# A two-image state-space scan: image 0 weighted by C on VectorE and summed with identity products, image 1 with its states transposed to tokens

## The chip, the cores and the metric

The kernel runs on one core of a Trainium2 chip. A core has five engines with an instruction queue each: TensorE (PE, matrix products; its weight loads are listed as PEld), VectorE (DVE), ScalarE (ACT), GpSimd (POOL) and SyncE (SP, which here only issues DMA transfers). An engine works through its queue in order: an instruction that waits holds up everything behind it on that engine. Data lies in SBUF (128 partitions); products land in PSUM, which has 8 banks of 128 x 512 floats and which POOL does not read here. The metric is device time in microseconds (us), the median over several runs. Everything is float32.

## The reference

The network takes x of shape (2, 128, 64, 64): two images, 128 channels, 4096 positions. In order: a group of deformable convolutions with a fuse convolution (called L0 conv below), a router with 8 experts (L0 FFN), a selective-scan mixer (L1 conv) and a last expert layer (L1 FFN). The change lies in the mixer's scan. For each image, with 256 inner channels d, 16 states n and positions t = 0..4095, the scan is

```
h[d,n,t] = exp(delta[d,t] * A[d,n]) * h[d,n,t-1] + delta[d,t] * u[d,t] * B[n,t]
y[d,t]   = sum over n of  C[n,t] * h[d,n,t]   +  D[d] * u[d,t]
out      = (y * gate[d,t]) projected from 256 to 128 channels, added to the layer's input
```

u and the gate come from convolutions of the normalised input; delta, B and C are products of u with small matrices.

## The kernel before

**Pieces and units.** The scan works on pieces of LC = 512 positions: 8 pieces per image, 16 in all. One unit is one scan instruction: 128 channels (one of two halves) by 512 positions for one state n. A piece has 2 x 16 = 32 units, and the loop in `scan` (L1550 onwards) goes over 512 units, ordered by (piece, half, state). Units 0 to 255 are image 0, units 256 to 511 image 1.

**One unit u.** ScalarE makes the decay `da` = exp(delta * A) into a PSUM bank (L1587, two units ahead, two banks). A DMA on SP's queue copies one row of B, broadcast over 128 partitions, to `bcb` (L1598, 256 KB, 8 buffers, about six units ahead). POOL makes the drive `db` = du * bcb (L1580, three units ahead). VectorE runs the scan `h` = scan(da, db) from the kept state (L1668); POOL then copies the last column of h to the state (L1677, one unit later). To weight h by C and sum over n, h is turned so that positions lie on the partitions: `turn` makes four 128 x 128 transposes on TensorE into a PSUM bank `ht` (listed under the helper's line L120, one unit later). There C[n, t] is one number per partition, and `weigh` multiplies it in two units later: for image 0, VectorE takes the first two blocks of 128 in one instruction (L1614) and ScalarE the other two (L1616, one each); for image 1, VectorE one block, ScalarE three. `add` then transposes the four blocks back, summing them in a PSUM bank `py` (L1625, three or four units later). The sum begins with the product of diag(D) and u (L1622). When all 16 states are in, `gate` multiplies by the gate on VectorE (L1637), and `project` (L1700 onwards) does the output projection.

**Preparing a piece.** While a piece is scanned, `prepare` makes the next one's delta, du, gate and rows of B and C in small steps, two steps per unit. It is a generator; `gap(n)` is n empty steps. It uses all engines, and loads xc, zc and sab through SP's queue.

**What lies beside the scan.** The order of the work is written out by hand: each engine's instructions are issued in the order in which the Python code makes them. During image 0's units, a second generator `rest` makes image 1's remaining earlier work: the fuse convolution (units 0 to 34, L875 and L877), the FFN (units 35 to 97, L1028, L1035 and L1044), the mixer's convolutions (units 98 to 190, L1234, L1247, L1269) and channel statistics (units 191 to 225, L1326). After each unit a fixed amount of `rest` is issued, so which step lies beside which unit is fixed by weights in the code. Image 1's units have only the preparation of the next piece and weight loads for the last layer beside them.

**Memory.** PSUM during the scan: two banks `da`, two `ht`, one `py`, and three shared by everything else (tag `m`). SBUF pools are stacked; work tiles of prepare share the tag `wk` with three buffers, and `xr` of project uses it too.

Of the kernel before, what the change touches and what calls it, by code (L numbers as in the profile page):

```python
# [19 lines left out]
P = 128  # L20
B = 2
# [189 lines left out]
class L0Conv:  # L211
# [690 lines left out]
    def residual(self, b, g, keep, sp):  # L902

        nc, cut = self.env.nc, slice(g * 512, (g + 1) * 512)
        row = lambda name: sp.tile([P, 512], F32, name=name, tag="t", bufs=7)
        xr, fa, fn = row("xr"), row("fa"), row("fn")
        nc.sync.dma_start(out=xr, in_=self.env.d["x"][b, :, cut])
        nc.sync.dma_start(out=fa, in_=self.fd[b][:, cut])
        for _ in range(3):
            yield  # L910
        for py in range(2):
            nat = view(fn, py * W, [(2 * W, 4), (2, 32), (1, 2)])
            phases = view(fa, py * 256, [(32, 4), (1, 32), (P, 2)])
            nc.scalar.activation(nat, phases, AF.Relu, bias=keep[:, 1:2], scale=keep[:, 0:1])
        yield
        yield
        return xr, fn


class L0Ffn:  # L920
# [26 lines left out]
    def group(self, b, g, residual, norm, x2, sp, pp):  # L947
        env, nc = self.env, self.env.nc
        bank = lambda shape, name: pp.tile(shape, F32, name=name, tag="m")
        row = lambda name: sp.tile([P, GT, C], F32, name=name, tag="t", bufs=7)  # L950
# [132 lines left out]
BCB = 8  # L1083
# [31 lines left out]
class L1Conv:  # L1115
# [315 lines left out]
    def taps(self, b, k, xc, xs, zz, sa, sp, bank, wk):  # L1431

        env, nc, halves = self.env, self.env.nc, range(2)
        if k == 0:
            self.wd = self.room().tile([P, 2, 4, P], F32, name="wd")
            for h in halves:
                for t in range(4):
                    nc.scalar.mul(self.wd[:, h, t, :], env.ident, self.w1[b][:, h, t : t + 1])
                yield
# [27 lines left out]
    def prepare(self, b, k, sp, pp, res):  # L1467
# [17 lines left out]
        yield from gap(11)  # L1485
        zz = sp.tile([P, 2, LC], F32, name="zc")
# [5 lines left out]
        xs = sp.tile([P, 2, LC], F32, name="xs")  # L1492
        if b:
            yield from self.taps(b, k, xc, xs, zz, sa, sp, bank, wk)
        else:
            yield from self.tap_sums(b, xc, xs, zz, sa, wk)
# [7 lines left out]
        bc = self.dp.tile([DS, LC], F32, name=f"bc{b}_{k}", tag=f"bc{b}_{k}")  # L1504
        nc.sync.dma_start(out=bc, in_=xd[8 : 8 + DS, :])
        res.update(bc=bc)
        yield
        pt = bank([P, GT, 40], "pt")
        for j in range(GT):
            nc.tensor.transpose(pt[:, j, :], xd[:, j * P : (j + 1) * P], env.ident[0:40, 0:40])  # L1510
        yield
        ct = sp.tile([P, GT, DS], F32, name="ct")
        nc.scalar.copy(ct, pt[:, :, 8 + DS :])
        res.update(ct=ct)
# [36 lines left out]
    def scan(self, sp, ps, pp, rest, ahead):  # L1551
# [20 lines left out]
        units = [(k, half, n) for k in range(B * NK) for half in range(2) for n in range(DS)]  # L1572
        pieces, das, dbs, rows, hs, hts, ws = {0: res}, {}, {}, {}, {}, {}, {}

        def drive(u):

            if u < len(units):
                k, half, n = units[u]
                dbs[u] = sp.tile([P, LC], F32, name="db", bufs=AHEAD + 1)
                nc.gpsimd.tensor_tensor(dbs[u], pieces[k]["du"][:, half, :], rows.pop(u), ALU.mult)  # L1580

        def decay(u):
            if u < len(units):
                k, half, n = units[u]
                das[u] = ps.tile([P, LC], F32, name="da")
                dl = pieces[k]["dl"][:, half, :]
                nc.scalar.activation(das[u], dl, AF.Exp, scale=self.A[:, half, n : n + 1])  # L1587

        fetched = 0

        def fetch(u):
            nonlocal fetched
            while fetched <= min(u, len(units) - 1):
                k, half, n = units[fetched]
                if "bc" not in pieces.get(k, {}):
                    break
                rows[fetched] = sp.tile([P, LC], F32, name="bcb", bufs=BCB)
                nc.sync.dma_start(out=rows[fetched], in_=pieces[k]["bc"][n].partition_broadcast(P))  # L1598
                fetched += 1

        adds, py = deque(), {}

        def turn(u):
            hts[u] = ps.tile([P, GT, P], F32, name="ht")
            h = hs.pop(u)
            transpose4(nc, env.ident, hts[u], [h[:, j * P : (j + 1) * P] for j in range(GT)])

        def weigh(u):
            k, half, n = units[u]
            ct, ht = pieces[k]["ct"], hts.pop(u)  # L1610
            ws[u] = sp.tile([P, GT, P], F32, name="w", bufs=4)
            cut = 2 if k < NK else 1
            by = ct[:, 0:cut, n : n + 1].to_broadcast([P, cut, P])
            nc.vector.tensor_tensor(ws[u][:, 0:cut, :], ht[:, 0:cut, :], by, ALU.mult)  # L1614
            for j in range(cut, GT):
                nc.scalar.activation(ws[u][:, j, :], ht[:, j, :], AF.Copy, scale=ct[:, j, n : n + 1])  # L1616

        def add(u):
            k, half, n = units[u]
            if n == 0:  # L1620
                py[k] = ps.tile([P, LC], F32, name="py", bufs=1)
                nc.tensor.matmul(py[k], dg[:, half, :], pieces[k]["xs"][:, half, :], start=True, stop=False)  # L1622
# [11 lines left out]
        def gate(u):  # L1634
            k, half, n = units[u]
            y = pieces[k]["zz"][:, half, :]
            nc.vector.tensor_tensor(y, y, py.pop(k), ALU.mult)  # L1637
# [4 lines left out]
        def flush(u):  # L1642
            while adds and adds[0][0] <= u:
                adds[0][1](adds.popleft()[2])
# [7 lines left out]
        for u, (k, half, n) in enumerate(units):  # L1652
            state = states[k // NK]
            if k and half == 0 and n == 5:
                side.todo.appendleft(project(k - 1))
            last = n == DS - 4 and half == 1
# [6 lines left out]
            fetch(u + BCB - 2)  # L1663
            if k >= NK and u % 24 == 12:
                ahead()

            hs[u] = sp.tile([P, LC], F32, name="h", bufs=3)
            nc.vector.tensor_tensor_scan(  # L1668
                hs[u], das.pop(u), dbs.pop(u), state[:, half, n : n + 1], ALU.mult, ALU.add
            )  # L1670
            if last:
                side.drain()
                fetch(u + BCB - 2)
            drive(u + AHEAD)

            if keep:
                nc.gpsimd.tensor_copy(*keep)  # L1677
            keep = state[:, half, n : n + 1], hs[u][:, LC - 1 : LC]
            decay(u + 2)
            if u:  # L1680
                turn(u - 1)
            if u > 1:
                weigh(u - 2)
            flush(u)
            adds.append((u + (4 if n == 0 else 3), add, u))
            if n == DS - 1:
                adds.append((u + 4, gate, u))
# [12 lines left out]

    def project(self, b, k, ys, sp, pp):

        nc = self.env.nc
        xr = sp.tile([P, 2, LC], F32, name="xr", tag="wk", bufs=3)[:, 0, :].rearrange("p (j c) -> p j c", j=GT)
# [19 lines left out]
    def run(self, after, ahead):  # L1724
# [4 lines left out]
        with (  # L1729
            tc.tile_pool(name="scs", bufs=2) as sp,  # L1730
            tc.tile_pool(name="scp", bufs=2, space=PSUM) as ps,
            tc.tile_pool(name="scm", bufs=3, space=PSUM) as pp,
        ):
            self.dtw = sp.tile([8, 256], F32, name="dtw", bufs=1)
# [250 lines left out]
def metaformer_kernel(ctx: ExitStack, tc: tile.TileContext, d: dict, out: bass.AP):  # L1985
# [6 lines left out]
    with tc.manual_schedule(engines={ET.PE, ET.DVE, ET.Activation, ET.Pool, ET.SP}), ExitStack() as l0:  # L1992
        mixer = L1Conv(env, dp, keep, x2, x3)
        mixer.room = lambda: ctx.enter_context(tc.tile_pool(name="wd", bufs=1, side="right"))
# [104 lines left out]
```

## Time and profile before

| | us |
|---|---|
| median of 7 runs | 7614.09 (7600.16 to 7626.24) |
| the profiled execution | 7606.2 |
| its span on the core | 7604.4 |
| from the span's start to the first scan | 5775.5 |
| image 0's units 0 to 255 | 1015.2 |
| image 1's units 256 to 511 | 562.4 |
| after the last scan's start | 251.3 |

The times in the profile are from the span's start. A group of instructions is named by line, engine, operation and tiles; "busy" is the time in which it ran, "idle before" the time for which the engine stood still just before it, with the instruction that ended the wait. "A <- B" in a list of waits means that A waited for B, with the total time, the number of waits and the longest. A float32 product of 512 columns appears as two records on TensorE, a transpose of 128 columns as one.

The first 5700 us hold the deformable convolutions of both images, with POOL's gathers, and are not touched except for one buffer count (the FFN's shared row tiles).

### The profile page before, as it was taken

To read this page: it belongs to the slowest core of one execution; us is meant where nothing else is said; L and a number is where in the kernel's file an instruction comes from. 1 tells how busy PE (TensorE), PEld (TensorE's weight loads), DVE (VectorE), ACT (ScalarE), POOL (GpSimd) and SP (SyncE) were. 2 spreads that over 40 slices of the span, in tenths; PEclk is the share of its full clock that TensorE was granted. 3 is DMA by queue.
4 is the path that set the end of the run, shared out by engine and by line. 5 is a ranking of instruction groups with operands and counts; after the bars stand their busy time and mean duration, and the time that the engine had idled before them with its cause. 6 is when DMAs were issued, how large, how long until landed. Compare 5 with 4: busy or idle time off the path is not lost.

```text
span 7604.4 us, 72120 instructions
## 1 busy us (share of the span) xinstructions
PE 5227.2 (69%) x22497; PEld 3287.0 (43%) x22497; DVE 5808.8 (76%) x6710; ACT 2248.1 (30%) x4642; POOL 5056.3 (66%) x5062
## 2 busy tenths in 40 slices
PE   4677677777777775756666776666556788867778
PEld 3444444444444442323333453434223567755544
DVE  5878788888888887788888877777875777578782
ACT  1211111111111111311111221111116776768770
POOL 3767677777777777777777776766774344567850
PEclk8887788888888887888888887778777888888889
DMA  7886767776777767877777777777765224455444
GB/s 215 261 278 210 215 210 217 210 223 204 222 213 217 217 207 249 281 230 211 227 213 218 230 223 234 217 242 214 232 203 188 98 91 130 133 153 158 157 149 155
DMA packets 667321, 1550.06 MB, mean 204 GB/s; under 512 B 181668, under 2 KB 230988, under 8 KB 666940
## 3 DMA queue, kind: packets, MB, share of 16 engines
q0 software_dynamic: 307200, 1006.88, 43.9%
q1 hardware_dynamic: 330812, 490.87, 20.6%
q10 hardware_dynamic: 28928, 47.70, 1.7%
q8 instruction: 182, 2.98, 0.2%
q14 instruction: 199, 1.63, 0.1%
HBM read 1436.70 MB, written 110.84 MB: 204 GB/s over the span
## 4 chain that ended last, share of the span: by engine, by line
PE 43%; issue 18%; another core or an unknown queue 15%; ACT 8%; DVE 8%; POOL 4%; DMA 3%; SPq 1%; ACTq 0%; DVEq 0%; POOLq 0%
PE out L799 18%; PE pst L120 6%; PE po L428 6%; POOL v L731 2%; PE ps L1247 2%; ACT st L779 2%; POOL db L1580 2%; DVE v L772 2%; DVE h L1668 1%; PE ps L1234 1%; PE pfo L875 1%; ACT w L1616 1%; PE px L1028 1%; PE ht L120 1%
## 5 line engine op out<-in xcount | busy, mean ns | idle before, releaser
L731 POOL DMA_INDIRECT v<-table,idx x3840 | 4059.2, 1057 | 1619.6 <-issue 1048.8
L772 DVE TENSOR_TENSOR v<-v,pw 128x2048 f32<-128x2048 f32 x960 | 2192.2, 2284 | 612.8 <-DMA v<-table,idx 408.9
L799 PE MATMUL out<-st,regw 128*128 128x512 f32 x3840 | 2234.4, 707 | 244.7 <-issue 189.7
L779 ACT COPY st<-pst 128x512 f32<-128x512 f32 x960 | 556.0, 586 | 4378.1 <-remote 2190.5
L120 PE MATMUL pst<-ident,v 128*128 128x128 f32 x3840 | 720.2, 312 | 1076.4 <-issue 863.5
L774 DVE TENSOR_TENSOR v<-v 128x1024 f32<-128x1024 f32 x960 | 1176.8, 1226 | 33.0
L799 PEld LDWEIGHTS out<-st,regw 128*128 128x128 f32 x3840 | 790.2, 228 | 905.7 <-issue 841.8
L120 PEld LDWEIGHTS pst<-ident,v 128*128 128x128 f32 x3840 | 514.8, 160 | 1460.1 <-issue 1192.0
L1580 POOL TENSOR_TENSOR db<-du,bcb 128x512 f32<-128x512 f32 x512 | 669.5, 1308 | 515.8 <-DVE h L1668 388.1
L1668 DVE TENSOR_TENSOR_SCAN h<-da,state,db 128x512 f32<-128x512 f32 x512 | 652.6, 1275 | 85.9 <-ACT da L1587 52.4
L775 DVE TENSOR_TENSOR v<-v 128x512 f32<-128x512 f32 x960 | 664.3, 692 | 33.0
L120 PE MATMUL ht<-ident,h 128*128 128x128 f32 x2048 | 365.1, 307 | 237.4 <-ACT w L1616 209.1
L428 PE MATMUL po<-wa,win 128*128 128x147 f32 x2112 | 388.9, 306 | 114.8 <-issue 112.2
L428 PEld LDWEIGHTS po<-wa,win 128*128 128x128 f32 x2112 | 340.7, 205 | 231.9 <-issue 231.3
L1587 ACT ACTIVATE da<-delta,w_A_log 128x512 f32<-128x512 f32 x512 | 359.7, 703 | 228.6 <-DVE h L1668 225.2
L120 PEld LDWEIGHTS ht<-ident,h 128*128 128x128 f32 x2048 | 263.0, 157 | 367.2 <-ACT w L1616 302.7
L1616 ACT ACTIVATE w<-ht,ct 128x128 f32<-128x128 f32 x1280 | 383.9, 371 | 22.4 <-DVE w L1614 22.4
L1614 DVE TENSOR_TENSOR w<-ht,ct 128x256 f32<-128x256 f32 (+1 forms) x512 | 174.3, 340 | 230.9 <-PE ht L120 229.1
L1625 PE MATMUL py<-ident,w 128*128 128x128 f32 x2048 | 340.8, 297 | 0.0
L1234 PE MATMUL ps<-ipw,hs 128*120 128x128 f32 x1408 | 212.8, 309 | 151.3 <-ACT X L1181 98.4
L1234 PEld LDWEIGHTS ps<-ipw,hs 128*120 128x120 f32 x1408 | 199.1, 215 | 205.1 <-ACT X L1181 115.5
L1625 PEld LDWEIGHTS py<-ident,w 128*128 128x128 f32 x2048 | 276.3, 157 | 23.6 <-issue 23.3
(327 smaller groups left out, 5294.2 us busy)
## 6 DMA issues: line engine op xcount, KB each, us to landing
bcb<-bc SPq DMA_DIRECT2D x512, 256.0 KB
regw<-in_regw SPq DMA_DIRECT2D x192, 640.0 KB
v<-table,idx POOLq DMA_INDIRECT x3840
yd<-ys ACTq DMA_DIRECT2D x128, 256.0 KB
yc<-yd SPq DMA_DIRECT2D x16, 2048.0 KB
wt<-in_weight SPq DMA_DIRECT2D x32, 1024.0 KB
tm<-pos SPq DMA_DIRECT2D x32, 720.0 KB
pos<-zero SPq DMA_DIRECT2D x48, 240.0 KB
```

What stands on the lines that cost most here:

```text
L120: nc.tensor.transpose(ps[:, j, :], s, ident)
L428: m()
L731: self.env.nc.gpsimd.indirect_dma_start(out=v[:, j, :], out_offset=None, in_=self.table[b], in_offset=bass.IndirectOffsetOnAxis(ap=idx[:, ...
L772: nc.vector.tensor_tensor(v4, v4, w, ALU.mult)
L774: nc.vector.tensor_tensor(up, up, v4[:, :, 2:4, :], ALU.add)
L775: nc.vector.tensor_tensor(v4[:, :, 0, :], v4[:, :, 0, :], v4[:, :, 1, :], ALU.add)
L779: nc.scalar.copy(st, pt.rearrange("p j t -> p (j t)"))
L799: nc.tensor.matmul(self.out[half], self.regw[t // CH][:, t % CH, half * P : (half + 1) * P], st, start=first, stop=last,)
L1234: nc.tensor.matmul(ps[:, k, :], patch, own[o], start=True, stop=True)
L1580: nc.gpsimd.tensor_tensor(dbs[u], pieces[k]["du"][:, half, :], rows.pop(u), ALU.mult)
L1625: nc.tensor.matmul(py[k][:, j * P : (j + 1) * P], w[:, j, :], env.ident, is_transpose=True, start=False, stop=n == DS - 1 and j == GT - 1,)
L1668: nc.vector.tensor_tensor_scan(hs[u], das.pop(u), dbs.pop(u), state[:, half, n : n + 1], ALU.mult, ALU.add)
```

## The change

- **Units of image 0** are ordered (piece, state, half), so that both halves of a state follow each other; image 1 keeps (piece, half, state).
- **Image 0's weighting.** The scan writes its result over `da`, in PSUM. VectorE multiplies it by a broadcast row of C into an SBUF tile `sc` (6 buffers), and TensorE adds it to `py` with one 512-column product by the identity, two units later. The turn, the weighing and the transposes back are gone for image 0; two sums (one per half) run side by side. The state is copied by ScalarE, since it is read from PSUM.
- **Image 1's weighting** is as before.
- **PSUM tags.** `da` has a third bank in image 0 (tag `y`, which is image 1's `py`); image 0's two `py` and image 1's two `ht` share the tag `x`.
- **bcb** becomes a tile of two rows (512 KB, 5 buffers): B and C of one state for image 0, used by both halves, and B of two states for image 1. One transfer serves two units. For image 0, prepare stores both B and C (two small transfers), and no longer makes `ct`.
- **Prepare** starts 5 steps earlier (`gap(6)` for `gap(11)`). `zc` has a third buffer for image 1; `xs` has one buffer per pool; a pool `scx` for image 1's extra tiles is opened when its first piece is prepared. `project` is put in one unit earlier for pieces up to 8, and `xr` has a buffer of its own.
- The tile `h` of image 1 has 6 buffers (before 3), `w` 5 (before 4); the FFN's row tiles 8 (before 7). `wd` moves from its own pool to the scan's.

```diff
-        row = lambda name: sp.tile([P, GT, C], F32, name=name, tag="t", bufs=7)
+        row = lambda name: sp.tile([P, GT, C], F32, name=name, tag="t", bufs=8)
...
-BCB = 8
+BCB = 5
...
-        yield from gap(11)
-        zz = sp.tile([P, 2, LC], F32, name="zc")
+        yield from gap(6)
+        own = self.own(b, sp)
+        third = b and k % 3 == 2
+        zz = (own if third else sp).tile([P, 2, LC], F32, name="zc", bufs=1 if third else 2)
...
-        xs = sp.tile([P, 2, LC], F32, name="xs")
+        xs = (own if k % 2 else sp).tile([P, 2, LC], F32, name="xs", bufs=1)
...
-        bc = self.dp.tile([DS, LC], F32, name=f"bc{b}_{k}", tag=f"bc{b}_{k}")
-        nc.sync.dma_start(out=bc, in_=xd[8 : 8 + DS, :])
+        bc = self.dp.tile([DS, LC] if b else [DS, 2, LC], F32, name=f"bc{b}_{k}", tag=f"bc{b}_{k}")
+        if b:
+            nc.sync.dma_start(out=bc, in_=xd[8 : 8 + DS, :])
+        else:
+            for s in range(2):
+                nc.sync.dma_start(out=bc[:, s, :], in_=xd[8 + s * DS : 8 + (s + 1) * DS, :])
...
-        units = [(k, half, n) for k in range(B * NK) for half in range(2) for n in range(DS)]
+        units = [(k, n, half) for k in range(NK) for n in range(DS) for half in range(2)]
+        units += [(k, n, half) for k in range(NK, B * NK) for half in range(2) for n in range(DS)]
+        first = NK * 2 * DS
...
-                das[u] = ps.tile([P, LC], F32, name="da")
+                third = u < first and u % 3 == 2
+                das[u] = ps.tile([P, LC], F32, name="da", tag="y" if third else "da", bufs=1 if third else 2)
...
-                rows[fetched] = sp.tile([P, LC], F32, name="bcb", bufs=BCB)
-                nc.sync.dma_start(out=rows[fetched], in_=pieces[k]["bc"][n].partition_broadcast(P))
+                bcb[i] = sp.tile([P, 2, LC], F32, name="bcb", bufs=BCB)
+                bc = pieces[k]["bc"]
+                nc.sync.dma_start(out=bcb[i], in_=(bc[n : n + 2] if k >= NK else bc[n]).partition_broadcast(P))
...
+        def start(k, half, key, tag, bufs):
+            py[key] = ps.tile([P, LC], F32, name="py", tag=tag, bufs=bufs)
+            nc.tensor.matmul(py[key], dg[:, half, :], pieces[k]["xs"][:, half, :], start=True, stop=False)
+
+        def identity(u):
+            k, n, half = units[u]
+            nc.tensor.matmul(py[k, half], env.ident, scs.pop(u), start=False, stop=n == DS - 1)
...
-            hs[u] = sp.tile([P, LC], F32, name="h", bufs=3)
-            nc.vector.tensor_tensor_scan(
-                hs[u], das.pop(u), dbs.pop(u), state[:, half, n : n + 1], ALU.mult, ALU.add
-            )
+            s = das.pop(u)
+            h = s if u < first else sp.tile([P, LC], F32, name="h", tag="sc", bufs=6)
+            nc.vector.tensor_tensor_scan(h, s, dbs.pop(u), state[:, half, n : n + 1], ALU.mult, ALU.add)
...
             if keep:
-                nc.gpsimd.tensor_copy(*keep)
-            keep = state[:, half, n : n + 1], hs[u][:, LC - 1 : LC]
+                keep()
+            to, end = state[:, half, n : n + 1], h[:, LC - 1 : LC]
+            keep = functools.partial(nc.scalar.copy if u < first else nc.gpsimd.tensor_copy, to, end)
             decay(u + 2)
-            if u:
-                turn(u - 1)
-            if u > 1:
-                weigh(u - 2)
+            if u < first:
+                scs[u] = sp.tile([P, LC], F32, name="sc", bufs=6)
+                nc.vector.tensor_tensor(scs[u], h, bcb[i][:, 1, :], ALU.mult)
+                if now == 0:
+                    adds.extend((u + 3, start, k, h, (k, h), "x", 2) for h in range(2))
+                adds.append((u + (3 if now == 0 else 2), identity, u))
+                if n == DS - 1:
+                    adds.append((u + 4, gate, k, half, (k, half)))
+            else:
+                if u == first:
+                    flush(u + 4)
+                hs[u] = h
+                if u > first:
+                    turn(u - 1)
+                if u > first + 1:
+                    weigh(u - 2)
+                adds.append((u + (4 if n == 0 else 3), back, u))
...
-        xr = sp.tile([P, 2, LC], F32, name="xr", tag="wk", bufs=3)[:, 0, :].rearrange("p (j c) -> p j c", j=GT)
+        xr = sp.tile([P, GT, C], F32, name="xr", bufs=1)
```

## The prediction

> **What bounds the kernel now.** I read the instruction groups, then busy time by stretch, the waits of image 0's stretch, and two timelines. Only the scan, 5775 to 7353 us, is changed much, so I cut there: fuse convolution (units 0 to 34), FFN (35 to 97), convolutions (98 to 190), statistics (191 to 225), image 0's scan without the other work (226 to 255), image 1's scan, the rest.
>
> ```profile
> L1668 DVE TENSOR_TENSOR_SCAN h<-da,state,db 128x512 f32<-128x512 f32 x512 | 652.6, 1275 | 85.9 <-ACT da L1587 52.4
> ...
> L1614 DVE TENSOR_TENSOR w<-ht,ct 128x256 f32<-128x256 f32 (+1 forms) x512 | 174.3, 340 | 230.9 <-PE ht L120 229.1
> ```
>
> The scan itself rarely stands still; the weighting behind it waits 229 us for the transposes.
>
> ```profile
> 5775.50:5908.00 132.50, 103.40 (x416) 57.71 (x417) 80.42 (x118) 109.30 (x194) 69.81 (x83) 0.90 0.59 203
> 5908.00:6227.50 319.50, 251.26 (x1218) 169.61 (x1216) 238.34 (x498) 241.18 (x542) 126.67 (x149) 0.84 0.26 86
> 6227.50:6577.20 349.70, 299.99 (x2290) 264.10 (x2290) 216.78 (x234) 246.31 (x525) 180.66 (x221) 0.84 0.46 127
> 6577.20:6708.80 131.60, 96.68 (x813) 87.97 (x810) 88.36 (x116) 81.36 (x186) 69.46 (x86) 0.88 0.59 166
> 6708.80:6790.70 81.90, 57.36 (x292) 41.46 (x293) 59.08 (x83) 56.34 (x120) 52.55 (x70) 0.76 0.41 133
> 6790.70:7353.10 562.40, 408.31 (x2394) 301.76 (x2392) 448.55 (x584) 460.32 (x1136) 454.63 (x564) 0.85 0.49 156
> ```
>
> Columns: stretch, length, busy time of PE, PEld, DVE, ACT, POOL, granted clock, DMA share, GB/s. No engine is full. TensorE is nearest in the convolutions (300 of 350); in the FFN PE, ACT and DVE are within 13 us of each other. These stretches lose time by engines waiting for one another. Image 0's waits:
>
> ```profile
> POOL db L1580 <- DVE h L1668: 325.5, 114, 8.6
> DVE w L1614 <- PE ht L120: 174.8, 87, 8.7
> ACT da L1587 <- DVE h L1668: 157.7, 78, 12.1
> ...
> POOL db L1580 <- DMA bcb<-bc: 105.7, 29, 9.1
> PE ht L120 <- ACT w L1616: 81.2, 49, 12.2
> DVE ws L1035 <- PE px L1028: 51.3, 17, 7.2
> ```
>
> A ring: VectorE waits for TensorE's transposes, TensorE for ScalarE's weighting (it empties the bank), ScalarE and POOL for VectorE's scan. The change cuts it.
>
> **Step 1: VectorE does more.** Where image 0 runs freely, a unit is scan and weighting:
>
> ```profile
> 6784.64 1.28 DVE L1668 TENSOR_TENSOR_SCAN h<-da,state,db 128x512 f32<-128x512 f32 x1
> 6785.83 0.40 DVE L1614 TENSOR_TENSOR w<-ht,ct 128x256 f32<-128x256 f32 x1
> 6786.14 1.28 DVE L1668 TENSOR_TENSOR_SCAN h<-da,state,db 128x512 f32<-128x512 f32 x1
> ```
>
> 1.51 us, each starting 0.08 before the last ends. The new product has 512 columns, one operand from PSUM: the gate L1637 is that, 0.682 us. It reads the scan's result, so the overlap goes (dependent neighbours on L1530 and L1532 lie 0.04 apart): 1.27 + 0.04 + 0.68 - 0.08 = 1.91 us. Extra: 0.40 x 256 = +102 us of VectorE. The scan now writes PSUM; no scan here does. The nearest row, the copy into PSUM of L764 (128x480, 0.658 us), has the 0.16 us beyond its columns that L775 has in SBUF (128x512, 0.692), so I add nothing; the bounds are 0 and 0.16 x 256 = 41 us.
>
> **Step 2: TensorE does the same.** Eight transposes become one product of 512 columns. In the chain, in the fuse convolution:
>
> ```profile
> 5897.07 0.44 PE ht L120 x4
> 5897.51 0.44 PE py L1625 x4
> 5897.95 1.72 PE pfo L875 x4
> ```
>
> 0.88 us for the eight, and 1.72 for two 512-column products: 0.86 each. No change. The Trainium skill speaks against this: "TensorE: Matmul & The Clock Gate", Terms, holds transpose mode four times faster for float32, and "FP8 and Floating Point Precision", TensorE Precision Notes, gives a true float32 product four passes. By these pages 512 columns at four passes against 1024 at one would be 1.76 us against 0.88, an estimated +225 us of TensorE and a clearly slower kernel; the row decides. What goes is the wait for ScalarE, 81 us.
>
> **Step 3: ScalarE and POOL do less.** ScalarE loses 506 instructions of L1616, 156 us, and gains 256 one-column copies; the nearest row is L1315 from PSUM, 0.20 us: +51. POOL loses the state copies, 71 us, all beside its 325 us of waiting for the scan: worth nothing. The decay gets a third bank: the one for unit u+2 waits for the product of u-1 rather than the scan of u, so ScalarE may run a unit further ahead.
>
> **Step 4, stretch by stretch.** VectorE's change is 0.40 per unit minus its wait for transposes (174.8 split as below), held by what comes late next.
> - Fuse, 34 units: +14 - 32 = -18. But TensorE keeps 2.6 us per unit (the chain above), and ScalarE's 2.53 (decay 0.58, weighting 0.54, two L877 1.41) falls by 0.34, or 12 us in all. I take -8; bounds -18, +14.
> - FFN, 64 units: +26 - 3. In its 17 waits on L1035 (51 us) the 0.40 is absorbed: -7. TensorE's 20.5 us of this stretch's wait for ScalarE delayed those px; half returns: -11. Sum +5; bounds -25, +26.
> - Convolutions, 93 units: +37 - 114 = -77 for VectorE, but TensorE has the same 300 us to run. Of its 50 idle, 13 were the wait on L1616, and others are waits for ScalarE, which is lighter; half goes: -25. Bounds -50, +37.
> - Statistics, 36 units: +14 - 19 = -5; bounds -27 (all of TensorE's wait there), +14.
> - Alone, 31 units: +12 - 6 = +6; bounds 0, +12.
>
> Sum: -8 + 5 - 25 - 5 + 6 = **-27 us**.
>
> **Step 5: image 1** keeps its operations. With three zc buffers, zc and sab no longer wait in SP's queue behind project's store; POOL stood 20.2 us for sab (L1446). With six h buffers the scan no longer waits for the state copy, 19.5 us. VectorE, ScalarE and POOL are each near 80%, and losses come with prepare's long operations, which stay. I take a fifth: -8; bounds -40, and +10 (waits for bcb, 9.0 us now, doubled by larger transfers).
>
> **Step 6: queues.** SP issues half as many bcb transfers of twice the size. For image 0 each buffer is held until VectorE has used C: 10 rows, but a reach of about five units instead of eight; POOL's 105.7 us of waiting for bcb can grow, though it is three units ahead. Image 0's zc load now stands ahead of xr on SP and waits until project has read the older zc, so xr lands late; the add L1720 waits, with the scan behind it. One such wait in the chain is "DMA xr<-x", 4.94 us: between 0 and 7 x 4.94 = 35. Project's products lie two units before the add; I take +5. The single xs buffer makes ScalarE wait for the D product (bounds 0 and 8 x 1.3, one scan each); it is issued in the same unit: 0. Two small bc stores for one, the absent ct and its transposes, the 512 KB first bcb, the wd pool and the eighth FFN row: 0, each under 2 us beside POOL's gathers or the 80 us in which the first piece is prepared; a few us either way if that cover is gone.
>
> **Sum:** -27 - 8 + 5 = -30 us on the profiled run's 7606.2, which is 8 below the median; on the median 7614.1 - 30 = **7584 us**, 0.4% faster.
>
> **Rivals.** About 0.2%, or 15 us, can be told from no change.
> - *VectorE becomes the bound (slower).* VectorE is what POOL and ScalarE wait for (325 and 158 us). If its wait on transposes was a wait for a busy TensorE in disguise, it comes back as a wait for a sum, a buffer of sc or a px, since TensorE streams the same columns. It decides once less than about 100 of the 175 us really go. With a third gone: +102 - 58 = +44, with steps 5 and 6 +41: 7655. For it: 683 us busy become 785 of 1015. Against: six sc buffers let VectorE run several units ahead of TensorE.
> - *The ring was the whole cost.* All engines pack better: -18 (fuse), -15 (FFN), -45 (convolutions), -15, +6, and -25 in image 1: -112, 7502. For it: 87 waits, up to 8.7 us; against: TensorE's 300 of 350.
> - *It cancels.* Some 60% of the wait goes, the rest pays for the product: within 15 us, 7614. That the change doesn't do what it says is excluded: the instruction order of the changed program has 256 products L1617 and 256 L1695 in image 0.
>
> **How the numbers follow.** Forecast (-15 to -71 us, own range 7543 to 7599) 0.34; the ring 0.13; cancelling 0.17; VectorE bound 0.36. The last is high because the FFN and the lone units have no cover for +102 us, and because the PSUM scan (41) and the late xr (35) both lie on its side. Faster 0.47, same 0.17, slower 0.36. The range goes from the ring's 7502 to the slower rival with a quarter gone (+102 - 44 - 3 = +55, 7669).
>
> **What would show it.** Right: scan still 1.27 us, L1695 near 0.68, L1617 about 0.86 a product; no wait of VectorE on transposes in image 0; the convolutions near 325 us with TensorE still near 300 busy; FFN not shorter. Wrong: a scan over 1.35 us; VectorE over 85% in the FFN; waits of L1695 for PE or bcb, or of the add for xr, by tens of us; image 1's scan longer than 572; TensorE's granted clock under 0.80 between 5775 and 6790.

## The result: 0.36% slower

The changed kernel takes 7641.5 us (median of 15 runs, 7629.7 to 7660.7) against 7616.9 for the kernel before (39 runs): a ratio of 1.0036, interval 1.0027 to 1.0045 (the two medians alone give 1.0032). The forecast was 7584, 0.4% faster; its sign was wrong. The profiled execution took 7626.9 us, its span is 7625.1, that is 20.7 more than before. The first scan starts at 5776.7 (before 5775.5), and the scan phase, first to last scan, is 16.7 longer; 2.8 lie behind it.

Busy time by stretch of the kernel after, in the prediction's stretches (units 0, 34, 98, 191, 226, 256, 511); columns: stretch, length, busy time of PE, PEld, DVE, ACT, POOL, granted clock, DMA share, GB/s.

```profile
5776.70:5900.80 124.10, 98.89 (x215) 41.60 (x216) 89.70 (x119) 97.25 (x161) 61.95 (x49) 0.90 0.61 217
5900.80:6197.40 296.60, 231.18 (x840) 124.82 (x840) 251.81 (x500) 217.19 (x484) 111.18 (x88) 0.86 0.29 93
6197.40:6551.60 354.20, 305.41 (x1746) 212.54 (x1747) 245.23 (x234) 213.62 (x429) 163.55 (x129) 0.84 0.46 128
6551.60:6693.60 142.00, 93.60 (x569) 65.91 (x568) 100.35 (x125) 69.61 (x148) 60.63 (x49) 0.85 0.50 150
6693.60:6785.90 92.30, 63.81 (x112) 20.12 (x110) 67.80 (x72) 44.58 (x86) 47.11 (x38) 0.78 0.30 100
6785.90:7371.00 585.10, 420.18 (x2374) 308.53 (x2374) 443.10 (x583) 480.25 (x1145) 458.34 (x564) 0.83 0.44 152
```

Fuse convolution and FFN are 8 and 24 us shorter than before, convolutions, statistics and the lone units 4, 6 and 16 longer (cut at the same units for both, see the table below; the prediction's later cuts lay up to 6 us early, so that its 131.6 us of statistics and 81.9 of lone units are 135.9 and 76.1), image 1 is 23 longer. No engine got much fuller: VectorE has 346 of 496 us in convolutions and statistics, TensorE 399. These stretches again lose time by waiting. The waits of image 0's stretch:

```profile
POOL db L1590 <- DVE da L1682: 414.0, 161, 14.7
ACT state L1689 <- DVE sc L1695: 122.4, 54, 11.8
POOL db L1590 <- DMA bcb<-bc: 101.4, 18, 11.4
DVE da L1682 <- ACT da L1598: 87.0, 35, 6.1
...
DVE xr L1750 <- DMA xr<-x: 38.7, 5, 10.1
...
ACT xs L1404 <- PE py L1613: 22.9, 6, 5.9
```

VectorE's 175 us of waiting for transposes are gone. In their place it waits 87 us for the decay (before 22.6) and 39 for `xr` (9.4). The same stretch for SP's queue, after and then before, the lines of the `zc` load alone:

```profile
SPq L1489 <- PE po L1740: 51.5, 7, 9.4
SPq L1489 <- DVE zc L1650: 49.0, 6, 14.1
```

```profile
SPq L1487 <- DVE zc L1637: 12.0, 1, 12.0
...
SPq L1487 <- PE po L1710: 6.3, 1, 6.3
```

The load of the next piece's `zc` now stands 100.5 us in SP's queue instead of 18.3, until the gate or the output projection of an older piece gives its buffer free. Everything issued behind it stands too. At the first piece of image 1, in the timeline (start, duration, engine and line, in brackets the idle time before it; POOL's last work before this was at 6796):

```profile
6783.59 0.42 SPq L1607 DMA_DIRECT2D bcb<-bc  x1
6800.22 0.37 SPq L1489 DMA_DIRECT2D zc<-zsd  x1
6800.64 0.46 SPq L1491 DMA_DIRECT2D sab<-sad  x1
6801.19 0.38 SPq L1607 DMA_DIRECT2D bcb<-bc  x1
6801.62 0.42 SPq L1735 DMA_DIRECT2D xr<-x  x1
...
6808.15 1.27 POOL L1590 TENSOR_TENSOR db<-du,bcb 128x512 f32<-128x512 f32 x1 [11.76 <-DMA bcb<-bc]
6808.70 0.69 DVE L1750 TENSOR_TENSOR xr<-xr,po 128x512 f32<-128x512 f32 x1 [7.75 <-DMA xr<-x]
```

After the load at 6783.59 nothing is issued on SP until `zc` at 6800.22. The loads of `bcb` and `xr` are issued right behind it and land 7 us later, while POOL and VectorE stand still; this first piece of image 1 takes 87.9 us, before 73.6. What comes late here seems to follow from an edit of one number, `gap(6)` for `gap(11)`, which starts `prepare`, and with it the load, two and a half units earlier. The experiments test that.

### The profile page after: what moved, and what is told of

It reads as the page before. It is cut to its first block, busy times and chain, and to the rows that moved or that the text cites. A ratio compares the mean times of both kernels' runs of the same rounds, so it can differ in the third digit from the quotient of the medians.

```text
span 7625.1 us, 67809 instructions
## 1 busy us (share of the span) xinstructions
PE 5198.2 (68%) x20929; PEld 3128.6 (41%) x20929; DVE 5868.2 (77%) x6710; ACT 2176.9 (29%) x4394; POOL 5039.7 (66%) x4806
## 5 line engine op out<-in xcount | busy, mean ns | idle before, releaser
L120 PE MATMUL pst<-ident,v 128*128 128x128 f32 x3840 | 710.4, 312 | 1144.8 <-issue 910.5
L120 PEld LDWEIGHTS pst<-ident,v 128*128 128x128 f32 x3840 | 511.6, 160 | 1529.9 <-issue 1232.6
L428 PE MATMUL po<-wa,win 128*128 128x147 f32 x2112 | 368.5, 300 | 83.5 <-issue 81.6
L1682 DVE TENSOR_TENSOR_SCAN da<-da,state,db 128x512 f32<-128x512 f32 x256 | 328.5, 1283 | 99.1 <-ACT da L1598 87.0
L1598 ACT ACTIVATE da<-delta,w_A_log 128x512 f32<-128x512 f32 x512 | 359.7, 703 | 69.8 <-DVE h L1682 58.0
L1682 DVE TENSOR_TENSOR_SCAN h<-da,state,db 128x512 f32<-128x512 f32 x256 | 326.2, 1275 | 46.9 <-ACT da L1598 46.8
L1234 PE MATMUL ps<-ipw,hs 128*120 128x128 f32 x1408 | 214.0, 310 | 183.9 <-ACT X L1181 87.8
L1617 PE MATMUL py<-sc,ident 128*128 128x512 f32 x512 | 310.8, 703 | 25.7 <-DVE sc L1695 25.6
L120 PE MATMUL ht<-ident,h 128*128 128x128 f32 x1024 | 187.3, 312 | 165.3 <-ACT w L1631 153.4
L1247 PE MATMUL ps<-tm,X 120*88 120x48 f32 x2048 | 225.1, 284 | 89.6 <-ACT Y L1181 35.4
L1247 PEld LDWEIGHTS ps<-tm,X 120*88 120x88 f32 x2048 | 218.1, 192 | 149.7 <-issue 59.5
L1631 ACT ACTIVATE w<-ht,ct 128x128 f32<-128x128 f32 x768 | 228.6, 384 | 24.3 <-DVE w L1629 24.1
```

The costliest lines, as they stand in the source:

```text
L120: nc.tensor.transpose(ps[:, j, :], s, ident)
L1234: nc.tensor.matmul(ps[:, k, :], patch, own[o], start=True, stop=True)
L1247: nc.tensor.matmul(ps[:, c, :], X[:, ch + c0 + c, :], t[:, :, c0 % TG + c], start=True, stop=True)
L1682: nc.vector.tensor_tensor_scan(h, s, dbs.pop(u), state[:, half, n : n + 1], ALU.mult, ALU.add)
```

## The experiments

Each ratio is to the kernel before in runs taken beside it on the same chip. In the first such group of runs (gap7, xr_early, gap11, before_gap6) the kernel before took 7265.7 us, since the phase ahead of the scan was some 340 us shorter there, for a reason not looked into; the scan was not. The stretches below, from scan start to scan start in the profiled execution, compare across all groups ("alone" is units 226 to 255); two executions of one kernel (the change and after_again, gap11 and gap11_again) differ by 1 and 7 us in the sum.

| us | fuse | FFN | conv. | statist. | alone | image 0 | image 1 | sum | ratio, interval |
|---|---|---|---|---|---|---|---|---|---|
| before | 132.5 | 321.0 | 349.7 | 135.9 | 76.1 | 1015.2 | 562.5 | 1577.7 | 1 |
| the change | 124.1 | 296.6 | 354.2 | 141.9 | 92.3 | 1009.1 | 585.2 | 1594.3 | 1.0036 (1.0027-1.0045) |
| after_again | 125.3 | 297.8 | 350.4 | 144.3 | 92.9 | 1010.7 | 582.5 | 1593.2 | 1.0036 (1.0025-1.0047) |
| gap11 | 123.4 | 297.9 | 344.4 | 124.8 | 83.5 | 974.0 | 557.4 | 1531.4 | 0.9935 (0.9920-0.9951) |
| gap11_again | 121.9 | 303.1 | 345.1 | 126.5 | 83.7 | 980.3 | 557.9 | 1538.3 | 0.9954 (0.9937-0.9971) |
| before_gap6 | 133.0 | 321.1 | 381.1 | 155.4 | 85.4 | 1076.0 | 641.7 | 1717.7 | 1.0161 (1.0145-1.0176) |
| gap7 | 122.2 | 300.7 | 362.6 | 150.0 | 86.9 | 1022.4 | 565.4 | 1587.8 | 1.0021 (1.0007-1.0036) |
| xr_early | 123.9 | 295.8 | 356.2 | 141.2 | 89.7 | 1006.8 | 577.3 | 1584.1 | 1.0029 (1.0015-1.0042) |
| zc3_sc5 | 123.9 | 296.6 | 344.7 | 142.1 | 89.3 | 996.6 | 577.0 | 1573.6 | 1.0005 (0.9995-1.0016) |
| zc3_sc5_gap7 | 122.3 | 301.0 | 359.0 | 137.9 | 79.5 | 999.7 | 551.4 | 1551.1 | 0.9962 (0.9947-0.9977) |
| xs2_sc5 | 123.3 | 300.1 | 354.7 | 141.7 | 92.7 | 1012.5 | 584.7 | 1597.2 | 1.0030 (1.0019-1.0042) |
| gap10 | 121.7 | 291.6 | 336.2 | 129.6 | 87.1 | 966.2 | 573.0 | 1539.2 | 0.9946 (0.9932-0.9960) |
| gap10_11 | 122.8 | 296.2 | 332.4 | 131.2 | 84.0 | 966.6 | 558.2 | 1524.8 | 0.9913 (0.9896-0.9929) |
| zc3_sc5_gap10_7 | 121.9 | 291.4 | 335.9 | 125.9 | 78.7 | 953.8 | 554.1 | 1507.9 | 0.9902 (0.9886-0.9919) |
| zc3_sc5_b4_gap7 | 128.7 | 301.1 | 364.9 | 137.0 | 80.8 | 1012.5 | 564.0 | 1576.5 | 0.9988 (0.9978-0.9998) |
| zc3_xs2_sc5_b4_gap7 | 128.9 | 301.2 | 346.2 | 134.1 | 81.2 | 991.6 | 563.4 | 1555.0 | 0.9973 (0.9962-0.9984) |
| g11_half_product | 123.1 | 299.3 | 342.9 | 122.1 | 77.7 | 965.1 | 558.3 | 1523.4 | 0.9939 (0.9923-0.9956) |
| g11_half_identity | 122.3 | 296.8 | 337.3 | 131.5 | 82.0 | 969.9 | 558.1 | 1527.9 | 0.9927 (0.9910-0.9943) |

### Is it the early start?

gap11 and gap7 edit the change, before_gap6 the kernel before:

```diff
-        yield from gap(6)
+        yield from gap(11)
```
```diff
-        yield from gap(6)
+        yield from gap(7)
```
```diff
-        yield from gap(11)
+        yield from gap(6)
```

> The changed kernel with gap(11), as in the kernel before: zc and sab are issued after project has read the old zc, so they hold nothing on SP's queue, and the number of steps is odd. Theory A: both parts go; image 1's scan back to 562 us or less, no VectorE wait for xr over 10 us in image 0, the time 30 to 55 us under 7641, so about the same as before or faster. Theory B: within 8 us of 7641, still slower than before by 25.

> The kernel before with gap(6) for gap(11) and nothing else. Theory A: it takes both losses without any change of the scan: 14 more table loads and VectorE waits for xr in both images (zc has two buffers there too); 20 to 60 us slower than before. Theory B: within 8 us of before.

> The changed kernel with gap(7) for gap(6): prepare half a unit later, an odd number of steps as in the kernel before. Theory A (the loss comes from the earlier start of prepare, in two parts): in image 1 the two sigmoid steps of a piece fall into one unit again, so the 14 table loads that the changed kernel has too many there (18 us of ScalarE) go; image 1's scan falls from 585 to about 576 us, its first piece keeps its 88 us, and the time falls by 6 to 15 us from 7641. Theory B (VectorE is the bound, C's product is the loss): no change, within 5 us of 7641.

With prepare's old start the change is 0.65% faster than the kernel before (0.46% in a second group of runs, gap11_again below), and the old scan with the early start is 1.61% slower than itself. Both go the way of theory A and beyond it: gap11 lies 0.8 to 1.0% under the change, 62 to 77 us where 30 to 55 were expected, and before_gap6 loses 120 us where 20 to 60 were. Of these, 79 lie in image 1's scan, where POOL now waits 87.8 us for `bcb` (before 9.0) and VectorE 59.6 for `xr`. So the early start is the loss, in both kernels, and the rest of the change together is a gain. It lies almost wholly in image 0 (35 to 41 us, against 5 in image 1), where the weighting was rebuilt; no run parts the weighting from the changed buffers and transfers that came with it. gap11 by stretch, from its second run:

```profile
5788.84:5910.78 121.94, 96.54 (x215) 39.97 (x216) 88.59 (x119) 96.99 (x161) 62.68 (x49) 0.93 0.62 215
5910.78:6213.90 303.12, 237.16 (x840) 126.27 (x840) 249.94 (x500) 217.09 (x484) 110.12 (x88) 0.86 0.28 91
6213.90:6559.03 345.13, 300.94 (x1727) 209.73 (x1728) 247.11 (x234) 212.86 (x429) 164.52 (x129) 0.83 0.47 129
6559.03:6685.54 126.51, 93.26 (x588) 66.03 (x587) 99.47 (x124) 69.62 (x149) 62.03 (x49) 0.87 0.61 177
6685.54:6769.28 83.74, 59.16 (x112) 19.92 (x110) 67.41 (x71) 42.39 (x84) 46.88 (x38) 0.80 0.33 104
6769.28:7327.23 557.95, 409.21 (x2374) 300.11 (x2374) 447.57 (x584) 459.73 (x1131) 453.24 (x564) 0.85 0.47 159
```

Against the change, 9 us are back in the convolutions, 15 in the statistics, 9 in the lone units and 27 in image 1. ScalarE in image 1 has 1131 instructions instead of 1145. The difference is table loads: ScalarE loads a table when it changes between Exp (the decay) and Sigmoid. Its groups in image 1, the change first, then before:

```profile
L1598 ACT ACT_TABLE_LOAD x14 | 18.0, 1283 | 0.3
L1456 ACT ACT_TABLE_LOAD x7 | 9.0, 1283 | 0.0
L1459 ACT ACT_TABLE_LOAD x7 | 9.0, 1283 | 0.1
```

```profile
L1456 ACT ACT_TABLE_LOAD x7 | 9.0, 1283 | 0.1
L1587 ACT ACT_TABLE_LOAD x7 | 9.0, 1283 | 0.1
```

`prepare` makes its two sigmoids (L1456, L1459) in neighbouring steps, and two steps are issued per unit. Eleven empty steps ahead put both into one unit, six put a decay between them: 14 more loads, 18 us. gap7 is odd again, and has 7 and 7, as gap11 has; its steady pieces of image 1 (units 288 to 511) take 481.9 us like gap11's 482.1, where the change takes 497.3. But as a whole it gains only 0.15%, since the convolutions and statistics of image 0 got 16 us longer.

### Is it the load in SP's queue?

xr_early issues the `xr` load at the piece's first unit, ahead of `zc`:

```diff
+            if k and now == 0:
+                self.residual((k - 1) // NK, (k - 1) % NK, sp)
...
-        nc.sync.dma_start(out=xr, in_=self.x2[b][:, k * GT : (k + 1) * GT, :])
```

> The changed kernel, with project's load of xr issued at the first unit of the piece, ahead of xc and zc on SP's queue; project's other steps stay where they are. Theory A: the waits of VectorE for xr (38.7 us in image 0, 7.7 us in image 1's first piece) go, that first piece falls from 88 to about 78 us, and the time falls by 20 to 45 us. POOL's wait for bcb of up to 11.8 us may stay, because zc still holds SP's queue. Theory B: within 8 us of 7641, because other VectorE waits take its place.

VectorE's 38.7 us of waiting for `xr` are gone; the wait for the decay grew from 87.0 to 103.6, and POOL still waits 98.7 for `bcb`. Ratio 1.0029, which its interval does not tell from the change's 1.0036, and 10 us of scan phase, 8 of them in image 1. Theory A's 20 to 45 us did not come: the wait that the prediction had named was for the most part a symptom. zc3_sc5 takes away what the load waits for, with after_again beside it:

```diff
-        zz = (own if third else sp).tile([P, 2, LC], F32, name="zc", bufs=1 if third else 2)
+        zz = sp.tile([P, 2, LC], F32, name="zc", bufs=3)
...
-                scs[u] = sp.tile([P, LC], F32, name="sc", bufs=6)
+                scs[u] = sp.tile([P, LC], F32, name="sc", bufs=5)
```

(and five `h` buffers, to make room)

> The changed kernel (gap(6)) with three zc buffers in both images, so that the zc load waits for nothing on SP's queue; to make room, sc and h have 5 buffers, not 6. Theory Q (the queue: SP stands 100 us at zc in image 0, and bcb, xr, the stores and loads of the convolutions stand behind it): image 0's units fall from 1009 to about 975 us, image 1's first piece from 88 to about 77 us, the rest of image 1 keeps its 14 table loads and its 497 us; the time is 35 to 50 us under the changed kernel, about 0.2% under before. Theory S (the early steps themselves: xs has one buffer, and ScalarE waits 23 us for the D product before it writes xs): less than 15 us gained.

> The changed kernel once more, on the chip of the next three runs: the same ratio to the kernel before, between 1.002 and 1.005, whatever the time of the chip's first 5400 to 5800 us is.

The two waits of L1489 are gone from SP's list. 0.31% comes back, 20.7 us of scan phase against the change (19.6 against after_again): 9.5 in the convolutions (5.7), 8.0 in the first piece of image 1 (87.9 to 79.9, the timeline above). Theory Q asked for 35 to 50. It is about a third of the loss against gap11, not all of it.

### Is VectorE or TensorE the bound instead?

These halve one operation on top of gap11:

```diff
-                nc.vector.tensor_tensor(scs[u], h, bcb[i][:, 1, :], ALU.mult)
+                nc.vector.tensor_tensor(scs[u][:, 0:256], h[:, 0:256], bcb[i][:, 1, 0:256], ALU.mult)
```
```diff
-            nc.tensor.matmul(py[k, half], env.ident, scs.pop(u), start=False, stop=n == DS - 1)
+            nc.tensor.matmul(py[k, half][:, 0:256], env.ident, scs.pop(u)[:, 0:256], start=False, stop=n == DS - 1)
```

> gap(11), and image 0's product by C covers 256 of 512 columns only (0.42 us for 0.69); the identity product reads those 256 columns twice, so TensorE's work stays. Left out: C on the second half of each piece's positions in image 0. Theory V (VectorE bounds image 0's 974 us): 69 us of VectorE less give 50 us or more. Theory T (TensorE bounds the convolutions): only the FFN and the lone units (about 95 units x 0.27) follow, 15 to 30 us, and the convolutions stay within 5 us of 344.

> gap(11), and image 0's identity product covers 256 of 512 columns: about 0.43 us less of TensorE per unit, 110 us in all; VectorE's work stays. Left out: the sum over states for half the positions of image 0. Theory T: the convolutions fall from 344 by 25 to 40 us (93 units x 0.43 = 40). Theory V: under 10 us there, and under 15 in all.

Neither moves the time by what its theory asks: 0.9939 and 0.9927, with gap11 at 0.9935 and 0.9954 (in other groups of runs). Theory V asked for 50 us or more from half the product; image 0 is 9 to 15 us shorter. Theory T asked for 25 to 40 us in the convolutions from half the identity product; they are 7 to 8 shorter. With half of C's product VectorE has 227 instead of 247 us of work in the convolutions, and the stretch takes 343 instead of 345; its wait for the decay rises to 116.3 us. Convolutions and lone units of half_product, then these and the statistics between them of half_identity:

```profile
6206.23:6549.15 342.92, 303.09 (x1728) 211.60 (x1728) 227.10 (x235) 212.50 (x429) 164.03 (x129) 0.83 0.46 130
...
6671.20:6748.94 77.74, 55.44 (x112) 19.04 (x110) 59.75 (x72) 42.32 (x84) 46.53 (x38) 0.84 0.35 112
```

```profile
6208.46:6545.74 337.28, 280.77 (x1738) 229.20 (x1739) 247.28 (x235) 213.01 (x429) 163.91 (x129) 0.75 0.48 133
6545.74:6677.23 131.49, 90.57 (x579) 77.67 (x577) 101.67 (x124) 68.81 (x149) 60.92 (x49) 0.73 0.57 169
6677.23:6759.20 81.97, 47.43 (x112) 21.77 (x110) 67.39 (x71) 42.27 (x84) 46.82 (x38) 0.65 0.33 106
```

Mostly the lone units, by 6 us, follow VectorE. "VectorE becomes the bound", the slower rival, is refuted, by this run and by gap11, which has the change's VectorE work and is faster than before: the sign was its, the cause was not. On TensorE the answer is weaker, since only 20 of the 40 us went from its busy time (last section).

### Do queue and parity add up to all of it?

zc3_sc5_gap7 has zc3_sc5's edits and gap(7); gap10 is the change with gap(10), an even number and yet late ("parity" is whether the number of empty steps is even or odd); xs2_sc5 gives `xs`, which ScalarE in the change waits for, a second buffer (with five `sc` and `h`):

```diff
-        xs = (own if k % 2 else sp).tile([P, 2, LC], F32, name="xs", bufs=1)
+        xs = sp.tile([P, 2, LC], F32, name="xs", bufs=2)
```

> The changed kernel with gap(11), a second time, on the chip of the three others: 0.9935 +- 0.0015 of the kernel before, image 1's steady pieces 482 us. It is the mark from which the three others are read.

> The changed kernel with gap(10): prepare starts one step, half a unit, earlier than with gap(11), and stays four steps later than in the change. It tells parity from earliness. Theory of the parity (an even number of steps puts prepare's two sigmoids into different units, with a decay between them): 14 more table loads of 1.283 us in image 1 (18 us of ScalarE), units 288 to 511 take 497 us instead of 482, image 0 stays within 5 us of gap(11), so 15 to 18 us or 0.0020 to 0.0024 above gap(11): 0.9955 to 0.996. Rival, only earliness counts (one step of five): a fifth of the 0.0101 between gap(6) and gap(11), about 0.0020, but spread over the convolutions and statistics of image 0, with image 1 at 485 or below and no more table loads.

> Both causes mended while prepare still starts four steps early: three zc buffers (the load no longer waits in SP's queue) and an odd number of steps (no more table loads in image 1). If the queue and the parity are all of the loss: 0.9935 to 0.9945, as with gap(11). If they only add up as measured one by one (0.0031 and 0.0015): 1.0036 - 0.0046 = 0.999, and some 40 us stay with the early start itself, in the statistics (above 135 us where gap(11) has 125) and the lone units, with ScalarE's wait for the single xs buffer (17 to 23 us) still in the list.

> The change with two xs buffers in the scan's pool for both images, and five sc and h buffers for six to make room; two zc buffers and gap(6) stay. ScalarE's wait for the D product before it writes xs (22.9 us, six times, in image 0) should be gone. If that wait is a third cause: 10 to 20 us, 1.001 to 1.0025. If it only stands in place of a wait that comes right after (ScalarE's decays wait for VectorE, VectorE for POOL, POOL for bcb behind the zc load): 1.003 to 1.004, with the decay's waits grown by as much.

- zc3_sc5_gap7 reaches 0.9962. Alone the two edits gave 0.0031 and 0.0015, together 0.0074: 43 us of scan phase against 21 + 6 (gap7's 6 are not clear of noise). The 16 us beyond the sum read as one wait hiding behind the other. Image 1 loses nothing any more: 551 us, less than gap11's 558. What is left, 19 to 26 us against the two runs of gap11, lies in image 0.
- xs2_sc5 removes ScalarE's 22.9 us and gains nothing that its interval shows, 1.0030. With the `zc` load still in the way, POOL still waits 98 us for `bcb` and 420 for the scan.
- gap10 was a surprise. Its 14 extra table loads are there (L1598 x14, L1456 x7, L1459 x7), and image 1 is 15 us longer than with gap11, as expected. But image 0 is 8 to 14 us shorter than in the two runs of gap11, and the ratio is the same. FFN, convolutions and image 1 of gap10:

```profile
5906.09:6197.66 291.57, 232.54 (x840) 124.07 (x840) 246.40 (x499) 216.91 (x484) 110.12 (x88) 0.88 0.30 95
6197.66:6533.90 336.24, 299.48 (x1727) 209.40 (x1728) 249.38 (x234) 212.62 (x429) 164.97 (x129) 0.84 0.49 133
...
6750.63:7323.64 573.01, 408.93 (x2374) 302.49 (x2374) 443.56 (x584) 481.36 (x1145) 450.62 (x564) 0.84 0.46 155
```

Image 0's pieces make their sigmoid elsewhere (one operation, L1421), so the table loads there hardly change (33 at L1598 in gap10, 32 in gap11_again). With the early start the even number is better in image 0 too (the change's 1009 us against gap7's 1022), though with three `zc` buffers by 3 us only. What it does better there is not known from these runs.

### The last two questions

gap10_11 takes the even number for image 0 and the odd one for image 1, zc3_sc5_gap10_7 does so with zc3_sc5's buffers:

```diff
-        yield from gap(6)
+        yield from gap(11 if b else 10)
```
```diff
-        yield from gap(6)
+        yield from gap(7 if b else 10)
```

> The changed kernel with gap(10) for image 0's pieces and gap(11) for image 1's. If parity is two separate effects, one per image: image 0 966 us as with gap(10), image 1 558 as with gap(11), scan phase 1524, 14 us below either: 0.993 of the kernel before. If the even number only pushes work from image 0 into image 1: 1538, 0.995.

> Three zc buffers, five sc and h buffers; gap(10) for image 0's pieces, gap(7) for image 1's. If what is left with the early start lies in image 0 alone: image 0 966 us, image 1 551, scan phase 1517, 0.992. If five sc buffers cost image 0 something, it is 975 or more: 0.9935 or above.

In gap10_11 image 0 takes gap10's 966 us and image 1 gap11's 558: the effects are separate, one per image. The ratio is 0.9913, and 0.9902 with the third `zc` buffer and the early start in image 1. The latter is the fastest version of the study, 7492.3 us against 7562.5 for the kernel before beside it. Its image 0 takes 953.8 us where 966 were expected. That is not explained: in gap10_11 the `zc` load waits for nothing in image 0 either, so differences of 10 us there need not have a named wait behind them.

zc3_sc5_b4_gap7 and zc3_xs2_sc5_b4_gap7 are zc3_sc5_gap7 with `BCB = 4` (for room), without and with the second `xs` buffer:

> The control for the next one: three zc buffers, five sc and h, gap(7), and four bcb buffers instead of five. Each bcb holds two units, so the reach falls from about five units to about four. If POOL's lead of three units is enough: 0.996 as with five, POOL's wait for bcb near 62 us. If not: that wait grows, by 20 us or more, and the ratio is 0.998 to 1.002.

> The control with two xs buffers in the scan's pool. ScalarE's wait for the D product (24 us in image 0) should be gone. If it was the remaining cause: image 0 980 us, 20 us or 0.0025 below the control. If other waits take its place: image 0 within 6 us of the control, ratio within 0.001 of it.

Waits of image 0, the control first:

```profile
POOL db L1590 <- DVE da L1682: 279.0, 104, 13.9
POOL db L1590 <- DMA bcb<-bc: 239.9, 40, 14.4
...
ACT xs L1404 <- PE py L1613: 18.8, 5, 4.8
```

```profile
POOL db L1590 <- DVE da L1682: 273.8, 102, 13.3
POOL db L1590 <- DMA bcb<-bc: 242.3, 44, 14.0
```

The wait for `xs` is gone, and image 0 is 21 us shorter, 19 of them in the convolutions (0.9973 against 0.9988, intervals that just overlap). So the single `xs` buffer, whose wait of 18.8 us goes, is a third cause, worth nothing that shows while the `zc` load is in the way, and once it is not, 21 us of image 0 in the profiled executions and 12 in the medians. That is about what zc3_sc5_gap7 lacks against gap11 in image 0 (19 to 26). The control also prices the reach of `bcb`: with four buffers POOL waits 240 us for it instead of 62, and the scan phase is 25 us longer.

## Why the prediction was wrong

The change without and with the early start, by the prediction's terms (us, change minus before; the middle column is gap11_again minus before):

| term | predicted | with the old start | as changed |
|---|---|---|---|
| fuse | -8 | -10.6 | -8.4 |
| FFN | +5 | -17.9 | -24.4 |
| convolutions | -25 | -4.6 | +4.5 |
| statistics | -5 | -9.4 | +6.0 |
| alone | +6 | +7.6 | +16.2 |
| image 1 (step 5) | -8 | -4.6 | +22.7 |
| queues (step 6) | +5 | in the rows above | in the rows above |
| sum | -30 | -39 | +17 |

- **Steps 5 and 6 failed.** The earlier start of `prepare` had no term of its own. Step 5 let image 1 keep its operations and gain 8; the start put 14 table loads into it and delayed its first piece, and it lost 23. Against gap11_again the first piece is 11.8 us longer and the other seven, with the table loads, 15.5; with the old start image 1 gained 5, so the step was right but for the start. Step 6 saw that the `zc` load would stand ahead of `xr` and wait for the older piece, but counted only `xr`, at +5 with 35 as a bound. Behind the same load stood `sab`, the `bcb` rows and the stores and loads of the convolutions, and removing the `xr` wait alone gave next to nothing. Together 100.5 us in that queue position (before 18.3) cost about 20 us by themselves.
- **The single `xs` buffer**, put at 0 "since it is issued in the same unit", waits 22.9 us in the change, more than the bound of 8 x 1.3. Beside the waiting `zc` load it costs nothing that shows, without it 12 to 21 us.
- **The FFN** was +5 and is -18 to -30 in every version of the change. I let half of TensorE's wait for ScalarE's weighting return. VectorE's wait for `px` halved (51.3 to 25.9), the whole wait for `w` went, and VectorE's busy time rose by 13.5, not 26. The **convolutions** were put at -25; with the old start they gave -5 (odd) to -13 (even), or -17 in gap10_11. TensorE kept its 300 us, as said, but most of its 50 idle us stayed (44 in gap11_again). That the sum with the old start, -39, comes near -30 is luck in part: the FFN was off by 23 us one way, the convolutions by 20 the other.
- **Step 1** was right in kind. Alone, a unit takes 1.99 us (1.93 to 2.00; predicted 1.91, before 1.51), so the extra is 0.48:

```profile
6758.05 1.28 DVE L1682 TENSOR_TENSOR_SCAN da<-da,state,db 128x512 f32<-128x512 f32 x1
6759.42 0.69 DVE L1695 TENSOR_TENSOR sc<-da,bcb 128x512 f32<-128x512 f32 x1
6760.03 1.28 DVE L1682 TENSOR_TENSOR_SCAN da<-da,state,db 128x512 f32<-128x512 f32 x1
```

  Writing to PSUM costs the scan 8 ns (first group; the second is image 1's, into SBUF), 2 us in all, so the upper bound of 41 was not needed:

```profile
L1682 DVE TENSOR_TENSOR_SCAN da<-da,state,db 128x512 f32<-128x512 f32 x256 | 328.5, 1283 | 99.1 <-ACT da L1598 87.0
...
L1682 DVE TENSOR_TENSOR_SCAN h<-da,state,db 128x512 f32<-128x512 f32 x256 | 326.2, 1275 | 46.9 <-ACT da L1598 46.8
```

- **Step 2** was right: over image 0's stretches TensorE's busy time went from 808.7 to 792.9 us (the sums of the windows before and after). The product takes 1.21 us of TensorE's busy time a unit (L1617, 310.8 us for 256), not the 0.86 of the chain, but the eight transposes took 1.37 (181.9 us on L120, 169.9 on L1625). The estimated 225 us that "TensorE: Matmul & The Clock Gate", Terms, and "FP8 and Floating Point Precision", TensorE Precision Notes, of the Trainium skill would have added did not come.
- **Step 3**: a decay bank more did not let ScalarE run ahead. VectorE's wait for the decay rose from 22.6 to 87.0 us, and it is 78 to 106 in the faster versions too. ScalarE now makes the state copies, which wait 122 us for VectorE (90 to 98 with the late start in image 0) and stand ahead of the next decay in its queue. What that costs was not measured.
- **The fuse term and the lone units** came out within 3 us with the old start. Of "the ring was the whole cost" little came: with the old start the whole change gains 39 to 46 us in the scan phase, not 112.

Of the signs named ahead, "image 1 longer than 572" and "the add for xr by tens of us" came true, and both pointed at the start of `prepare`, not at the new weighting. The granted clock under 0.80 came too, 0.78 in the lone units, but says nothing: before, it was 0.78 in the same units. Of the signs of being right, "FFN not shorter" and "convolutions near 325" failed.

Open: why an even number of empty steps saves 8 to 14 us of image 0 with the late start, why the third `zc` buffer shortens image 0 with the late start, and how the loss splits among the three causes, since they do not add up singly.

## What to carry to other kernels

An empty step is an edit like any other: list every instruction that it moves, with the buffer that each waits for, and what stands behind each in its queue. Where several late things hide behind one another, taking one away shows only a part of what it costs; take away two together before one is called harmless. Price the parts of a large change apart, since here a gain of 0.5 to 0.65% and a loss of 0.8 to 1% lay in one change.

## What the runs showed of the hardware

In one run TensorE's granted clock was lower when a part of its work was left out. With half of the identity product it was 0.75 in the convolutions, 0.73 in the statistics and 0.65 in the lone units, where gap11_again had 0.83, 0.87 and 0.80 (windows above). The identity product in the convolutions, gap11_again first:

```profile
L1617 PE MATMUL py<-sc,ident 128*128 128x512 f32 x186 | 116.1, 717 | 0.0
L1617 PE MATMUL py<-sc,ident 128*128 128x256 f32 x188 | 75.7, 500 | 0.0
```

It took 40 us less, as forecast, but TensorE's busy time fell only from 301 to 281 us: the other products took 20 us more. So leaving out work of TensorE understated here what that work costs at an unchanged clock, and such a run bounds a TensorE limit only from one side. What sets the clock is not shown: the busy share alone does not, since gap11_again's FFN, 78% busy, has 0.86 and half_identity's convolutions, 83% busy, have 0.75.
